# Two units of row lists behind each of three tiles, five listing steps in four expert slots, and two projections moved behind the second sorted tile

## The chip, the core and the metric

The kernel runs on one core of a Trainium2 chip. Its engines are TensorE (PE in the profile; its weight loads are PEld), VectorE (DVE), ScalarE (ACT), GpSimd (POOL) and SyncE (SP). [...] The metric is the device time of one execution in microseconds (us), less is better.

## What is computed

A block with two branches on the same normalised rows, for x of shape (2, 1024, 256):

```
xn = layernorm(x)
out = x + attention(xn) + experts(xn)
```

The attention branch splits every row into 16-channel tokens, projects them to q, k and v, and attends within windows of eight tokens, for half of the channels along one axis and for the other half along the other one, with a small convolution of v added; a projection and a layernorm follow. The expert branch is a mixture of experts:

```
scores = sigmoid(xn @ gate.T);  choose 6 of 16 experts per row (within the best 2 of 4 groups)
for e in experts: out += weight[:, e] * ((silu(xn @ gate_e.T) * (xn @ up_e.T)) @ down_e.T)
out += (silu(xn @ sg.T) * (xn @ su.T)) @ sd.T          # a shared expert for every row
```

An expert has 176 hidden units; there are 2048 rows.

## The kernel before

**Tiles and lists.** The routing is worked out on the chip. The 2048 rows are then sorted so that each of 16 tiles of 128 rows has six experts that most of its rows have chosen. A pair of experts over one tile is a unit of work of the kind "six"; a tile has three such units, and their down projections add up in one PSUM tile. Pairs of row and expert that those six experts do not cover are gathered into 14 lists of 128 rows with one expert each; a pair of lists is a unit of the kind "extra". `units()` (line 1013) lays out the 55 units: the three units of each tile in turn, and behind each of the tiles 7 to 13 one unit of lists.

**The main loop** (from line 1125) runs over `u`, a unit, and `q`, one of its two halves; a half is called an expert slot here, and `i = 2 * u + q` counts them. In slot order the program text issues: a sorted tile that is due (`sorted_tile`, `asked`), a step of the listing, the gathers of the next unit if that is one of lists, then `begun` (up projections of this unit, lines 867 to 870: PE products `pr_u`, Silu on ACT, a multiply on DVE into `hms`), `hidden` of the unit before (L881: three transposes, and an ACT copy), `finished` of the unit two before (down projections, L893 for tiles and L901 for lists, and an ACT copy into `ysum`), then attention steps, and one scatter. A scheduler then reorders instructions on each engine within what their dependences allow, so that the order of an engine is near to that of the text but not the same.

**Lists.** The listing (`lists_begun`) is a generator: three preparing steps, then one step for each of 26 possible lists, then `lists_ended`. A step for list n copies three columns on ACT (`spot`, L967, two buffers), makes two one-hot operands on POOL (L969, L970, in a ring of four), and two steps later a PE product adds it to `rows_of` (L960). One step is taken in every slot from i = 14 on. `lists_ended` writes the row numbers (`lists`, L977 on DVE), which the gathers read. `gathered` (L994) is an indirect DMA that POOL issues, 128 rows into one of the three `xg` buffers; the buffer is free again when the list has been transposed (`turned`, L1001) and its weight column read by the multiply L870. The sorted tiles used the same three buffers before (L827).

**Scatters.** Every finished tile and every finished list is added to the output by an indirect DMA with accumulation (`to_out`, L1008), issued by POOL, 30 in all. Each waits until the one before it has landed, since all write the same output tensor. The attention result is added by eight further DMAs of POOL (L1079).

**Attention steps.** `attention_steps()` yields steps with a cost on DVE and on PE. `walked` takes steps while the DVE count is behind the PE count times a pace. The four parts (two batches, two channel halves) consist each of eight projections (L675 on PE, four copies on ACT L677 to L680), sixteen large DVE operations (L688, L692, L709, L714) and eight transposes (L729); a last stage (L781 to L806) follows. Before the loop, `walked(FIRST_ROWS - LEAD)` takes the first steps of the first part ahead of the second sorted tile; each projection counts 0.3, and so does the gather of rows in front of them. The remaining products of the shared expert (L275, L284, L290) are put behind these by `meanwhile(100)`.

Of the kernel before, what the change touches and what calls it, by code (L numbers as in the profile page):

```python
# [22 lines left out]
P = 128  # L23
# [20 lines left out]
NX = 26  # L44
NL = 14
FIRST = 7
# [5 lines left out]
def csw_block_moe(ctx: ExitStack, tc: tile.TileContext, x, qkv_w, conv_w0, conv_b0, conv_w1, conv_b1,  # L52
# [20 lines left out]
    nc = tc.nc  # L73
# [78 lines left out]
    for c in range(16):  # L152
        n = sum(P // 2 if k % 2 == 0 else P for k in range(c)) + (((16 - c) * P - 1) / 2 if c % 2 == 0 else 0)
# [380 lines left out]
    for c in range(15, -1, -1):  # L534
        n = 16 - c
# [8 lines left out]
        for k in range(1, n):  # L544
            nc.tensor.matmul(down_[:, c + k : c + k + 1], lhsT=beats[:, k, :], rhs=less[:, c % 2 : c % 2 + 1], start=False,
                             stop=(c == 0 and k == 15))
# [25 lines left out]
    for n in range(2):  # L572
        nc.vector.tensor_tensor(ohp[:, 8 * n : 8 * n + 8], row_h.unsqueeze(1).to_broadcast(wide),
                                place[:, 1, 8 * n : 8 * n + 8].unsqueeze(2).to_broadcast(wide), ALU.is_equal)
        for c in range(8 * n, 8 * n + 8):
# [31 lines left out]
    extra = route.tile([NTL, E], F32, name="extra")  # L607
# [6 lines left out]
                     start=True, stop=True)  # L614
# [297 lines left out]
    listed = []  # L912

    def lists_begun():
        flagged = room_[:, 832:960].bitcast(BF16)
        behind = room_[:, 960:1024].bitcast(BF16)
        spot = room_[:, 1024:1280]
        spoti = [t.bitcast(I32) for t in (room_[:, 1280:1536], ysum[:, 7])]
        by_pair = flagged.rearrange("p (e t) -> p e t", t=NTL)
        nc.vector.scalar_tensor_tensor(by_pair, wsrt.rearrange("p t e -> p e t"), 0.0, kept, op0=ALU.is_gt, op1=ALU.mult)  # L920
        nc.vector.tensor_scalar(behind, row_h, part_no, None, op0=ALU.is_gt)
        before = ps_m.tile([P, 2, E * NTL], F32, tag="m", name="before")
        nc.tensor.matmul(before[:, 0], lhsT=behind, rhs=flagged, start=True, stop=True)
        nc.tensor.matmul(before[:, 1], lhsT=ones, rhs=flagged, start=True, stop=True)
        yield
        rows_, some, upto = small.tile([P, E], F32, name="rows_"), small.tile([P, E], I32, name="some"), begin[:, 1]
        nc.vector.tensor_reduce(out=rows_, in_=before[:, 1].rearrange("p (e t) -> p e t", t=NTL), axis=AX.X, op=ALU.add)
        nc.vector.tensor_scalar(some, rows_, P - 1.0, None, op0=ALU.add)
        nc.vector.tensor_scalar(some, some, 7, None, op0=ALU.logical_shift_right)
        nc.vector.tensor_copy(begin[:, 0], some)  # L930
        one_e = one_f.to_broadcast([P, E])
        nc.vector.tensor_tensor_scan(ends, one_e, begin[:, 0], 0.0, op0=ALU.mult, op1=ALU.add)
        nc.vector.tensor_tensor(begin[:, 0], ends, begin[:, 0], ALU.subtract)
        nc.vector.tensor_tensor_scan(upto, one_e, rows_, 0.0, op0=ALU.mult, op1=ALU.add)
        nc.vector.tensor_tensor(upto, upto, rows_, ALU.subtract)
        nc.vector.scalar_tensor_tensor(begin[:, 0], begin[:, 0], float(P), upto, op0=ALU.mult, op1=ALU.subtract)
        nc.vector.tensor_tensor_scan(spot, one_f.to_broadcast([P, E * NTL]), before[:, 1], 0.0, op0=ALU.mult, op1=ALU.add)
        nc.vector.tensor_tensor(spot, spot, before[:, 1], ALU.subtract)
        nc.vector.tensor_tensor(spot, spot, before[:, 0], ALU.add)
        wide = [P, E, NTL]  # L940
        nc.vector.tensor_tensor(spot.rearrange("p (e t) -> p e t", t=NTL), spot.rearrange("p (e t) -> p e t", t=NTL),
                                begin[:, 0].unsqueeze(2).to_broadcast(wide), ALU.add)
        yield
        nc.vector.tensor_copy(spoti[0], spot)
        nc.vector.tensor_scalar(spoti[1], spoti[0], 7, None, op0=ALU.logical_shift_right)
        nc.vector.tensor_scalar(spoti[0], spoti[0], P - 1, None, op0=ALU.bitwise_and)
        nc.gpsimd.memset(at_[:, :, 0:1], 0.0)
        for n in range(2):
            nc.scalar.copy(at_[:, n, 1:], spoti[n])
        nc.vector.tensor_tensor(at_[:, 2, 1:].rearrange("p (e t) -> p e t", t=NTL), by_pair,  # L950
                                of_f.unsqueeze(1).to_broadcast(wide), ALU.mult)
        listed.append(ps_t.tile([P, NX], F32, tag="y1", name="rows_of", padded_shape=[P, TB]))
        yield
        spots = {}
        for n in range(NX + 2):
            if n < NX:
                spots[n] = pair_listed(n)
            if n >= 2:
                spot = spots.pop(n - 2)
                nc.tensor.matmul(listed[0], lhsT=spot[:, 0:P], rhs=spot[:, P:], start=(n == 2), stop=(n == NX + 1))  # L960
            yield
        lists_ended()
        yield

    def pair_listed(n):
        spot = small.tile([P, 3], F32, name="spot", tag="spot")
        nc.scalar.copy(spot, at_[:, :, bass.ds(number(xrow[0:1, 0, n : n + 1], ACT, NTL * E), 1)].rearrange("p a n -> p (a n)"))  # L967
        spots = room_[:, 1024 + 80 * (n % 4) :][:, 0 : (P + NX) // 2].bitcast(F16)
        nc.gpsimd.tensor_scalar(spots[:, 0:P], row_h, spot[:, 0:1], None, op0=ALU.is_equal)  # L969
        nc.gpsimd.tensor_scalar(spots[:, P:], row_h[:, 0:NX], spot[:, 1:2], spot[:, 2:3], op0=ALU.is_equal, op1=ALU.mult)  # L970
        return spots

    def lists_ended():

        none = room_[:, 1500 : 1500 + NX]
        nc.vector.tensor_scalar(none, listed[0], 0.0, ROWS + 1.0, op0=ALU.is_equal, op1=ALU.mult)
        nc.vector.scalar_tensor_tensor(lists[:, 0:NX], listed[0], -1.0, none, op0=ALU.add, op1=ALU.add)  # L977

        over = room_[0:1, 0 : NX * E].rearrange("p (n e) -> p n e", e=E)
        of_list = room_[0:1, 500 : 500 + NX]  # L980
        nc.vector.tensor_tensor(over, ends[0:1].unsqueeze(1).to_broadcast([1, NX, E]),
                                number_f[0:1, 0:NX].unsqueeze(2).to_broadcast([1, NX, E]), ALU.is_le)
        nc.vector.tensor_reduce(out=of_list, in_=over, axis=AX.X, op=ALU.add)
        nc.vector.tensor_scalar(xrow[:, 2, 0:NX], of_list, E - 1.0, None, op0=ALU.min)
        nc.vector.tensor_copy(xrow[:, 1, 0:NX], number_f[0:1, 0:NX])

        some = small.tile([1, 2], F32, name="some_")
        nc.vector.scalar_tensor_tensor(some[:, 0:1], pairs_[0:1], NX + 0.5, pairs_[0:1], op0=ALU.is_gt, op1=ALU.mult)
        nc.vector.tensor_tensor(some[:, 0:1], some[:, 0:1], ends[0:1, E - 1 : E], ALU.max)
        nc.vector.tensor_scalar(left, some[:, 0:1], -float(NL), 0.0, op0=ALU.add, op1=ALU.max)  # L990
# [22 lines left out]
    def units():  # L1013

        six = [[("six", t, k) for k in range(0, TOPK, 2)] for t in range(NTL)]
        for t in range(NTL):
            yield from six[t]
            if FIRST <= t < FIRST + NL // 2:
                yield "extra", 2 * (t - FIRST), 0

    def expert_of(what, q, engine):
        kind, n, k = what
# [61 lines left out]
    of_tile = (0.75, 0.25)  # L1084
    END = 84
    in_walk = [4 * (16 * 2.3 + 3.3 + 2.5 + 1.5 + 1.4) + 0.6 + 8 * 1.4, 4 * 6.2 + 8 * 3.9]
    FIRST_ROWS, LEAD = 2.5, 12
    done = [float(-LEAD), 0.0]
    whole = [in_walk[n] + NTL * TOPK * of_slot["six"][n] + NL * of_slot["extra"][n] + NTL * of_tile[n] for n in range(2)]
    pace = (whole[0] - LEAD - END * of_slot["six"][0] / of_slot["six"][1]) / (whole[1] - END)  # L1090
# [28 lines left out]
    extras_, lists_ = extras_listed(), lists_begun()  # L1119
# [4 lines left out]
    for u in range(len(laid_out) + 2):  # L1124
        for q in range(2):
            i = 2 * u + q

            while tiles_sorted < NTL and 5 * (tiles_sorted - 2) <= 6 * (i - 2):
                sorted_tile(tiles_sorted)
                counted(of_tile)  # L1130
                tiles_sorted += 1
            while len(asked_for) < min(NTL, tiles_sorted + 3):
                asked()
            if i in (2, 4, 8) or i >= 14:
                next(extras_ if i < 14 else lists_, None)
            if u + 1 < len(laid_out) and laid_out[u + 1][0] == "extra":
                n = laid_out[u + 1][1] + q
                ahead[n] = gathered(lists[:, n : n + 1])
            if u < len(laid_out):
                if q == 0:  # L1140
                    fetched(u)
                begun_.setdefault(u, []).append(begun(laid_out[u], q, hms[:, u % 2]))
            if q == 1:
                if 0 <= u - 1 < len(laid_out):
                    hT_[u - 1] = hidden(hms[:, (u - 1) % 2])
                if 0 <= u - 2 < len(laid_out):
                    finished(laid_out[u - 2], hT_.pop(u - 2), wts[:, (u - 2) % 3], begun_.pop(u - 2))
            counted(of_slot[laid_out[min(u, len(laid_out) - 1)][0]])
            walked()
            if done_:  # L1150
                to_out(*done_.pop(0))
            while waiting:
                waiting.pop(0)()
# [73 lines left out]
```

## Time and profile before

| what | us |
|---|---|
| median of three runs (lowest, highest) | 449.53 (446.91, 451.74) |
| the profiled execution: its time | 448.94 |
| the profiled execution: its span | 447.2 |
| PE busy in the span | 393.4 |
| DVE, ACT, POOL busy in the span | 293.0, 215.6, 187.8 |
| scatters L1008: 30, busy on POOL in all | 51.0 |
| gathers L994: 14, busy on POOL in all | 21.2 |

The profile page shows for each engine the busy share in 40 equal slices of the span, then the chain of work that ended last, followed back from the last instruction, then the costliest groups of instructions with what ended the idle time before them. The timeline of an engine lists its instructions in order with the idle time before each and its releaser in square brackets. A table of windows gives the busy time of every engine in a stretch, and the clock that TensorE was granted there, as a share of full speed.

### The profile page before, as it was taken

What the parts mean: (1) busy time and instruction counts of PE and PEld (TensorE: products, weight loads), DVE (VectorE), ACT (ScalarE), POOL (GpSimd) and SP (SyncE); (2) the same over time, 40 slices, a digit from 0 to 9 for tenths busy, and PEclk for the clock granted to TensorE, in tenths of its full rate; (3) what the DMA queues carried; (4) which work ended last, traced back from release to release, by engine and by line L of the source; (5) the groups of instructions that cost most, each with busy time, mean ns of one, the idle gap of its engine ahead of it and who ended that gap; (6) DMA issues with size and microseconds to landing.
All of it is one profiled execution on the core that took longest, in us unless ns stands there. A gap on an engine that the chain in (4) does not pass through costs nothing. (4 is left out here: it accounts for less than half of the span.)

```text
span 447.2 us, 6291 instructions
## 1 busy us (share of the span) xinstructions
PE 393.4 (88%) x1668; PEld 247.4 (55%) x1669; DVE 293.0 (66%) x515; ACT 215.6 (48%) x535; POOL 187.8 (42%) x207
## 2 busy tenths in 40 slices
PE   0999999997887979898898899999899999999970
PEld 0445565655554646665565476566655555666750
DVE  4627958679997948979779599398992333322110
ACT  2955247462472355372462452735335777843220
POOL 7400000220556145886504235324542778791431
PEclk9999999998999999999999699999999999999995
DMA  8999942320423110121012133202331129347222
GB/s 236 314 290 328 272 170 42 48 82 12 86 70 85 22 20 22 33 38 39 22 24 45 52 60 65 44 20 63 85 58 38 22 65 141 74 70 101 44 33 24
DMA packets 40178, 37.56 MB, mean 84 GB/s; under 512 B 5300, under 2 KB 37616, under 8 KB 40112
## 3 DMA queue, kind: packets, MB, share of 16 engines
q0 software_dynamic: 11616, 13.52, 18.4%
q1 hardware_dynamic: 27472, 22.59, 16.6%
q10 hardware_dynamic: 1056, 1.05, 0.7%
q8 instruction: 15, 0.25, 0.2%
q14 instruction: 19, 0.16, 0.1%
HBM read 27.70 MB, written 12.45 MB: 90 GB/s over the span
## 5 line engine op out<-in xcount | busy, mean ns | idle before, releaser
L867 PE MATMUL pr_u<-w1s,xsT 128*128 x384 | 128.3, 468 | 2.7 <-DVE hms L870 2.1
L867 PEld LDWEIGHTS pr_u<-w1s,xsT 128*128 128x128 f32 x384 | 69.9, 190 | 39.3 <-issue 7.1
L1008 POOL DMA_INDIRECT out_dram<-ysum,lists x30 | 51.0, 1701 | 88.5 <-ACT ysum L1047 38.0
L869 ACT ACTIVATE sg<-pr_u 128x176 f32<-128x176 f32 x110 | 34.6, 317 | 83.1 <-PE pr_u L867 73.6
L870 DVE SCALAR_TENSOR_TENSOR hms<-sg,w,pr_u 128x176 f32<-128x176 f32 x96 | 37.4, 392 | 49.1 <-ACT sg L869 46.6
L688 DVE TENSOR_TENSOR pr<-qk 128x2048 f32<-128x2048 f32 x16 | 36.6, 2288 | 15.8 <-ACT qk L677 15.3
L709 DVE TENSOR_TENSOR pv<-s,v 128x2048 f32<-128x2048 f32 x16 | 36.6, 2286 | 4.2 <-ACT s L700 4.2
L692 DVE TENSOR_REDUCE s<-pr 128x256 f32<-128x2048 f32 x16 | 36.5, 2281 | 0.1
L714 DVE TENSOR_REDUCE o<-pv 128x256 f32<-128x2048 f32 x16 | 36.4, 2272 | 0.0
L293 POOL DMA_DIRECT2D out_dram<-ysum x4 | 3.7, 914 | 76.1 <-ACT ysum L291 76.1
L881 PEld LDWEIGHTS ph<-ident,hms 128*128 128x128 f32 x165 | 21.4, 141 | 19.8 <-issue 8.0
L994 POOL DMA_INDIRECT xg<-xw_d,lists x14 | 21.2, 1512 | 26.2 <-DVE hms L870 23.7
L881 PE MATMUL ph<-ident,hms 128*128 128x128 f32 x165 | 29.5, 276 | 2.2 <-DVE hms L870 1.7
L969 POOL TENSOR_SCALAR ysum<-row_h,spot 128x128 f16<-128x128 f16 x26 | 21.3, 825 | 23.4 <-PE rows_of L960 17.0
L827 POOL DMA_INDIRECT xg<-xw_d,lists x16 | 21.6, 1353 | 18.7 <-PE px__1007 L835 6.5
L893 PE MATMUL pr_y<-w2a,hT 128*128 x96 | 28.7, 380 | 0.0
L893 PE MATMUL pr_y<-w2b,hT 112*128 x96 | 28.7, 379 | 0.0
L893 PE MATMUL pr_y<-wts,hT 128*128 128x256 f32 x96 | 28.5, 379 | 0.0
L290 PE MATMUL py<-room 128*128 128x256 f32 x96 | 25.3, 402 | 2.5 <-DVE room L284 2.5
L883 ACT COPY hT<-ph 128x384 f32<-128x384 f32 x55 | 26.3, 479 | 1.9 <-PE ph L881 1.2
L675 PE MATMUL pq<-wq,rows 128*128 128x384 f32 x64 | 24.8, 503 | 2.5 <-ACT oT L731 1.4
L867 PE MATMUL pr_u<-w1s,xd 128*128 x56 | 21.8, 518 | 5.1 <-ACT xd L1003 4.6
(403 smaller groups left out, 703.6 us busy)
## 6 DMA issues: line engine op xcount, KB each, us to landing
w1s<-in_w_dram SPq DMA_DIRECT2D x22, 256.0 KB
wts<-in_w_dram SPq DMA_DIRECT2D x55, 64.0 KB
wts<-in_w_dram SPq DMA_DIRECT2D x55, 48.0 KB
xw_d<-xx SPq DMA_DIRECT2D x4, 544.0 KB
w2a<-in_w_dram SPq DMA_DIRECT2D x4, 512.0 KB
out_dram<-ysum POOLq DMA_DIRECT2D x4, 512.0 KB, 6.8
xr<-xw_d POOLq DMA_DIRECT2D x4, 512.0 KB
out_dram<-att POOLq DMA_DIRECT2D x8, 256.0 KB, 4.1
```

Source lines behind the costliest of these rows:

```text
L290: nc.tensor.matmul(py, lhsT=hms[k, m][:, P * c : P * c + P], rhs=w2h[:, m], start=(m == 0), stop=(m == 2))
L688: nc.vector.tensor_tensor(pr, q_.unsqueeze(3).to_broadcast(full), k_.unsqueeze(2).to_broadcast(full), ALU.mult)
L692: nc.vector.tensor_reduce(out=s[:, n : n + NW], in_=held.pop(n), axis=AX.X, op=ALU.add)
L709: nc.vector.tensor_tensor(pr, s[:, n : n + NW].unsqueeze(3).to_broadcast(full), v[:, br, m : m + NW].unsqueeze(2).to_broadcast(full), ALU. ...
L714: nc.vector.tensor_reduce(out=o[:, n : n + NW], in_=held.pop(n), axis=AX.X, op=ALU.add)
L867: nc.tensor.matmul(pu, lhsT=lhs[:, h, :], rhs=w1s[:, :, h, bass.ds(e * I, I)], start=(h == 0), stop=(h == 1))
L869: nc.scalar.activation(sg, pu[:, 0, :], AF.Silu)
L870: nc.vector.scalar_tensor_tensor(hm[:, 0:I], sg, w, pu[:, 1, :], op0=ALU.mult, op1=ALU.mult)
L881: nc.tensor.transpose(ph[:, s, :], units[:, P * s : P * s + P], ident)
L883: nc.scalar.copy(hT, ph)
L893: nc.tensor.matmul(py, lhsT=l_, rhs=r_, start=start and n == 0, stop=stop and n == 2)
L1008: nc.gpsimd.indirect_dma_start(out=out_rows, out_offset=bass.IndirectOffsetOnAxis(ap=index, axis=0), in_=ys, in_offset=None, bounds_check= ...
```

## The change

There are four edits.

1. `units()` puts one unit of lists behind tile 7 and two behind each of the tiles 8, 9 and 10. The number of units stays 55; the last 15 units are tiles 11 to 15 without lists between them. The two units of lists behind one tile are neighbours.
2. The listing takes a further step in every fourth slot (`i > 16 and i % 4 == 0`), five steps in four slots.
3. The product L960 for a list comes three steps behind its operands instead of two; the ring of four operands stays. With both edits, `lists_ended` is reached in slot 40 instead of 45; the first gathers are still put in slot 46 by the text.
4. `FIRST_ROWS` is 2.0 instead of 2.5: the steps before the loop stop after the gather of rows and six projections instead of eight.

Nothing is computed that was not computed before, and no operation is added or taken away.

```diff
-        for n in range(NX + 2):
+        for n in range(NX + 3):
             if n < NX:
                 spots[n] = pair_listed(n)
-            if n >= 2:
-                spot = spots.pop(n - 2)
-                nc.tensor.matmul(listed[0], lhsT=spot[:, 0:P], rhs=spot[:, P:], start=(n == 2), stop=(n == NX + 1))
+            if n >= 3:
+                spot = spots.pop(n - 3)
+                nc.tensor.matmul(listed[0], lhsT=spot[:, 0:P], rhs=spot[:, P:], start=(n == 3), stop=(n == NX + 2))
             yield
...
+        n = 0
         for t in range(NTL):
             yield from six[t]
-            if FIRST <= t < FIRST + NL // 2:
-                yield "extra", 2 * (t - FIRST), 0
+            for _ in range((t == FIRST) + 2 * (t > FIRST)):
+                if n < NL:
+                    yield "extra", n, 0
+                    n += 2
...
-    FIRST_ROWS, LEAD = 2.5, 12
+    FIRST_ROWS, LEAD = 2.0, 12
...
             if i in (2, 4, 8) or i >= 14:
                 next(extras_ if i < 14 else lists_, None)
+            if i > 16 and i % 4 == 0:
+                next(lists_, None)
```

## The prediction

> **What bounds the kernel now.** I read the 40 slices first, then the end of the chain, then the timelines of PE and POOL where PE stands still, and last the windows around those places. TensorE carries the span: 393.4 of 447.2 us busy, nearly without gaps from slice 1 on.
>
> ```profile
> PE   0999999997887979898898899999899999999970
> PEclk9999999998999999999999699999999999999995
> DMA out_dram<-ysum,lists 3%; POOL out_dram L1008 0%; POOLq L1160 0%; POOLq L1008 0%
> 432.75 0.60 PE L893 MATMUL pr_y<-w2b,hT 112*128 x2
> ```
>
> The chain that ends last is not TensorE's. Its last product ends at 433.35, and 13.85 us follow in which it has no work. POOL fills them:
>
> ```profile
> 397.91 4.79 POOL L1079 DMA_DIRECT2D out_dram<-att  x4
> 408.88 1.66 POOL L1008 DMA_INDIRECT out_dram<-ysum,lists  x1 [6.18 <-ACT sg L869]
> ...
> 435.08 1.54 POOL L1008 DMA_INDIRECT out_dram<-ysum,lists  x1 [1.91 <-DMA out_dram<-ysum,lists]
> 439.61 1.54 POOL L1008 DMA_INDIRECT out_dram<-ysum,lists  x1 [2.99 <-DMA out_dram<-ysum,lists]
> ```
>
> Eight scatters start between 408.88 and 439.61, 4.39 us apart, each waiting for the one before to land. The last sum was ready at about 434.3; its scatter started 5.3 us later, behind a backlog. From there to the end it is 7.59 us.
>
> Inside the span the largest late stop of PE is at the first lists:
>
> ```profile
> 240.64 1.55 POOL L1008 DMA_INDIRECT out_dram<-ysum,lists  x1 [17.68 <-ACT ysum L1047]
> 242.50 2.64 POOL L994 DMA_INDIRECT xg<-xw_d,lists  x1 [0.30 <-issue]
> 247.04 0.69 PE L1001 MATMUL px__2528<-ident,xg 128*128 128x128 f32 x2 [3.09 <-DMA xg<-xw_d,lists]
> 248.37 0.47 PE L1001 MATMUL px__2549<-ident,xg 128*128 128x128 f32 x1 [0.64 <-DMA xg<-xw_d,lists]
> 106.07 1.29 PE L290 MATMUL py<-room 128*128 128x256 f32 x4 [2.52 <-DVE room L284]
> ```
>
> The lists are written at 241.85 (L977), and the first gather stands behind a scatter that waited for its sum. The windows show what comes after such a stop (columns: busy us of PE, PEld, DVE, ACT and POOL, then the granted clock):
>
> ```profile
> 103.50:106.00 2.50, 0.05 (x1) 0.00 (x0) 2.50 (x3) 0.00 (x0) 0.00 (x0) 1.00 0.07 30
> 108.00:110.00 2.00, 2.00 (x5) 1.43 (x5) 1.98 (x3) 0.32 (x1) 0.00 (x0) 0.50 0.00 0
> 249.00:251.00 2.00, 2.00 (x4) 1.25 (x5) 0.43 (x1) 0.00 (x0) 0.00 (x0) 0.50 0.10 24
> ```
>
> **The change part by part**, against the profiled execution (448.94 us, 0.59 under the median). The order of each engine in the changed kernel is known from building it; durations are those of the trace before.
>
> *End.* With no lists behind tiles 11 to 15, only four scatters (tiles 12 to 15) stand behind the last attention DMAs instead of eight. Tiles take PE three units of 4.0 us (405.90 to 409.89), 12 us for each scatter of 4.39, so no backlog is left when PE ends. The last scatter starts 0.9 after PE's last product: 0.9 + 7.6 = 8.5 instead of 13.85, -5.3.
>
> *First lists.* The listing ends five slots sooner, the lists are written about four units before they are needed, and the first three gathers stand behind the scatter of tile 5, not of tile 6. The wait of 3.09 goes. So does what follows it: the first unit of lists took 8.77 us from its first transpose (247.04) to the next unit (255.81), the second 5.77 (268.19 to 273.96). Together -6.1.
>
> *Listing, five steps in four slots.* POOL's two operations take 0.825 + 0.689 = 1.51 on average, five of them and a share of a scatter about 8.8 us, against four slots of 2.2 us (44.2 us for ten units, 171.94 to 216.1). POOL would then have no slack, and ACT, which waits 23.1 us for it at L967 now, waits as often. Against that stand the later product (it waited 1.28 for POOL, once) and two and a half units fewer under listing, whose PE idles 6.3 us between 160.2 and 221. Bounds -3 and +4; I take 0, as this row has both in it.
>
> *Two projections later.* In the new order they stand between the products L290 of the shared expert. The second L688 on DVE needs the last of them: it started at 103.13 and can now start at about 108, some 4.7 us later after taking out the two operations that DVE does meanwhile. DVE has little room here (24.1 of 25 us busy from 100 to 125). Covered by the transposes L729 coming later in PE's order, by one transpose group, one and a half up projections and one unit's down projections, 3.5 us. The stop of 2.52 at L284 stays, shorter or longer by under 1. Bounds -2 and +4; taken +1, the difference. Its DMAs are the same.
>
> *Neighbouring units of lists.* This is the dear part. Four lists follow each other (2 to 5, 6 to 9, 10 to 13), and `xg` has three buffers. The gather of the fourth has to wait until DVE has multiplied the first; behind that gather, on POOL, stand the next scatters and gathers, and on PE everything waits for the fourth list's transposes. PE's order puts these 5.5 us after the first list's products (the rest of that unit, 270.32 to 273.96, then 1.85 for the third list's transposes and products). The gather needs 0.3 of issue, 0.95 to 2.8 on POOL, and 1.95 to land (245.45 + 0.97 to 248.37). If DVE multiplied at once, 0.8 after the products, it would land after 4.0 to 5.9: in time. Two things hold it up:
> - DVE is behind. In its new order three L709, three L714, one L703, L704 and L722 and six multiplies (3 x 2.29 + 3 x 2.28 + 1.21 + 0.94 + 0.69 + 6 x 0.3 = 18.4) stand between the Exp after list 1 and the multiply of list 2, and PE gets from list 1 to list 2 in 16.0 (1.5 + three units of 4.0 to 4.4 + 2.1). Exp ends some 4 us after list 1's products, so DVE is up to 6 late, less what PE itself waits for it. Before list 6 there are eight operations of 2.29, done 4.4 after PE's products.
> - POOL is behind. Before the gather of list 9 come the scatters of tile 8 and lists 2 to 5, before that of list 13 those of lists 6 to 9 and a memset (L757, about 1.3). Scatters with a sum ready stood 4.56 apart among the lists (283.75 after 278.81, for one). From the first of the four sums: 3 x 4.56 + 1.6 + 0.3 = 15.6 to the gather, 18.5 to 20.4 until it has landed; PE is at the fourth transposes after 4.4 + 4.0 + 5.8 + 2.0 - 0.6 = 15.6.
>
> That gives stops of 0 to 6 for list 5 (taken 3.0), 1.9 to 4.8 for list 9 (3.4), and 1.3 to 6 for list 13 (4.1, DVE alone gives 1.3): +10.5.
>
> *The clock after these stops.* In the rows above a stop of 2.5 us was followed by about 3.3 us at half clock (0.73, 0.50 and 0.92 in three windows of 2 us, 1.7 us lost), one of 3.1 by 2.4 us lost (8.77 - 5.77 - 0.64). [...]
>
> Sum: -5.3 - 6.1 + 0 + 1 + 10.5 + 6 = +6.1, so 448.94 + 6.1 = 455.0. What is hidden: the transfers `wts` of SP keep their number and their lead of a unit; the scatters of lists 10 to 13 fall into the attention stage, where POOL has 3.4 us of L801 and L806 in each step of about 6, and three buffers between; if that cover fails, +3.
>
> **The rivals.**
> - *The fourth gathers land in time* (not slower). If DVE reaches the first list's multiply within about 1.5 us of PE's products and the scatters follow each other faster, all three stops and their clock loss go: 448.94 - 5.3 - 6.1 + 1 = 438.5. It decides where the gather can start less than about 2 us after those products. For it: between the lists before, PE never waited for a gather except at the first. Against: there lists came two at a time with two or three units between, and POOL still waited up to 9.2 us for DVE before a gather:
>
> ```profile
> 298.38 2.82 POOL L994 DMA_INDIRECT xg<-xw_d,lists  x1 [9.20 <-DVE hms L870]
> ```
>
> - *Stops without the clock, or one of three missing*: 455.0 - 6 = 449, no change that shows. [...]
> - *Listing at POOL's limit*: ACT stands at L967 ahead of Silu, and PE waits for `hms` in most units under listing; with 4 more there, 459. Against: POOL idled 17 us waiting for PE in the listing before.
> - *The backlog stays*: if the scatters of lists 10 to 13 delay the attention DMAs past 420, the 5.3 are not gained: 460. Against: ten units of tiles follow.
>
> **How the numbers follow.** Stops as summed (or with the listing or backlog cases on top): 0.45, 455.0. Stops in part or without clock loss, near 449: 0.25. No stops, near 438.5, or one small one: 0.30. About 1% of 449.5 (445.0 and 454.0) is what a measurement can tell from no change here, since three runs spread over 4.8 us. Slower by over 1%: 0.45; within: 0.25; faster: 0.30. The range goes from 438, the rival on the other side, to 461, the sum with listing or clock at their upper ends; the likeliest case alone is 450 to 461.
>
> **What would show it.** POOL's last scatter starting about 1 us after PE's last product, and some 8.5 us from there to the end: the end is right. The first L1001 with no wait on its gather: first lists right. Waits of PE at L1001 for `xg` three times, at lists 5, 9 and 13, with POOL's gather before each released by DVE L870 or by a scatter, and clocks near 0.5 behind them: the dear part is right. If these waits are under 1 us, the prediction is wrong and the time is near 439. If PE idles over 8 us under listing, it is wrong about POOL's slack.

## The result and the profile after

The changed kernel takes 464.5 us (median of four runs, 464.11 to 466.25) against 449.49 us (446.91 to 451.74) for the kernel before on the same chip: 1.0374 times as long, 95% interval 1.0339 to 1.0408. The profiled execution took 466.25 us, the longest of the four; its span is 464.4 us, 17.2 more than before, where the medians stand 15.0 apart. 455.0 was predicted, with a range that ended at 461.

The span splits at the last product of PE. Before, it ended at 433.35 and 13.85 us followed; now it ends at 456.52 and 7.9 us follow. So the end of the kernel gained 5.9 us, and everything ahead of it lost 23.2. The timelines of PE and of POOL end with these lines, the last scatter 0.7 us behind the last product, where it stood 6.3 behind it before:

```profile
455.92 0.60 PE L893 MATMUL pr_y<-w2b,hT 112*128 x2
```

```profile
457.20 1.56 POOL L1008 DMA_INDIRECT out_dram<-ysum,lists  x1 [5.37 <-ACTq L1167]
```

PE and its clock in 40 slices, from the page of the changed kernel:

```profile
PE   0999999989787969779899986995974999999993
PEclk9999999999997999998999997997995999999998
```

Each slice is 11.6 us. The clock has a digit of 7 or less in four slices, counted from 1: in slice 13 (7), and in 25 (7), 28 (7) and 31 (5), where PE is low too (6, 5 and 4). PE's timeline has what lies there (in brackets the idle time before the instruction, and what ended it):

```profile
142.22 0.66 PE L835 MATMUL px__1371<-ident,xg 128*128 128x128 f32 x2 [4.37 <-DMA xg<-xw_d,lists]
...
251.97 0.38 PE L1001 MATMUL px__2528<-ident,xg 128*128 128x128 f32 x2
...
283.39 0.66 PE L1001 MATMUL px__2794<-ident,xg 128*128 128x128 f32 x2 [4.27 <-DMA xg<-xw_d,lists]
...
321.64 0.66 PE L1001 MATMUL px__3123<-ident,xg 128*128 128x128 f32 x2 [4.69 <-DMA xg<-xw_d,lists]
...
354.59 0.66 PE L1001 MATMUL px__3378<-ident,xg 128*128 128x128 f32 x2 [7.34 <-DMA xg<-xw_d,lists]
```

The last three are the fourth lists of the three rows of neighbours: `px__2794` is list 5, `px__3123` list 9, `px__3378` list 13, 16.3 us in all. `px__1371` is the gather of a sorted tile, 110 us ahead of the first lists; before, this wait was 1.72. The first lists (`px__2528`) no longer wait.

Each of the four pairs of transposes behind a stop took 0.66 us instead of 0.38: the granted clock has fallen (0.50 from 142.00 to 146.00, behind the first of them). The windows show it for the other three (columns as in the prediction: busy us of PE, PEld, DVE, ACT, POOL, then the granted clock), first inside the stop at list 5, then in the 6 us behind each of the three stops:

```profile
281.39:283.39 2.00, 0.00 (x0) 0.03 (x1) 1.83 (x3) 0.00 (x0) 1.28 (x2) 0.50 0.47 107
...
283.39:289.39 6.00, 6.00 (x19) 4.49 (x20) 0.40 (x1) 1.54 (x4) 1.24 (x2) 0.66 0.14 41
321.64:327.64 6.00, 6.00 (x20) 4.67 (x21) 1.97 (x4) 1.54 (x4) 2.32 (x2) 0.72 0.18 45
354.59:360.59 6.00, 6.00 (x18) 4.50 (x19) 0.40 (x1) 1.54 (x4) 0.00 (x0) 0.62 0.01 3
```

PE is busy all through these 6 us. Clocks of 0.66, 0.72 and 0.62 mean 2.0, 1.7 and 2.3 us lost, 6.0 for the three.

Where the gathers of lists 9 and 13 came from is in POOL's timeline:

```profile
300.65 3.40 POOL L1008 DMA_INDIRECT out_dram<-ysum,lists  x1 [8.98 <-ACT ysum L1057]
306.37 2.68 POOL L1008 DMA_INDIRECT out_dram<-ysum,lists  x1 [2.32 <-DMA out_dram<-ysum,lists]
311.99 2.20 POOL L1008 DMA_INDIRECT out_dram<-ysum,lists  x1 [2.93 <-ACT xd L1003]
316.33 1.56 POOL L1008 DMA_INDIRECT out_dram<-ysum,lists  x1 [2.14 <-DMA out_dram<-ysum,lists]
318.19 1.02 POOL L994 DMA_INDIRECT xg<-xw_d,lists  x1 [0.30 <-DVE s L699]
...
331.34 3.37 POOL L1008 DMA_INDIRECT out_dram<-ysum,lists  x1 [0.30 <-ACT ysum L1057]
337.12 2.51 POOL L1008 DMA_INDIRECT out_dram<-ysum,lists  x1 [2.42 <-ACT sg L869]
342.60 2.62 POOL L1008 DMA_INDIRECT out_dram<-ysum,lists  x1 [2.97 <-ACT xd L1003]
348.08 1.54 POOL L1008 DMA_INDIRECT out_dram<-ysum,lists  x1 [2.85 <-ACT sg L869]
349.06 1.52 POOL L757 MEMSET xe<- 128x1024 f32 x1
350.75 1.07 POOL L994 DMA_INDIRECT xg<-xw_d,lists  x1 [0.17 <-issue]
```

The multiply that frees the buffer of list 9 ended at 315.4 on DVE; its gather started at 318.19, behind four scatters. For list 13 it ended at 344.1, and the gather started at 350.75, behind four scatters and a memset. Six of the eight scatters took 2.2 to 3.4 us; 22 of the kernel's 30 took 1.54 to 1.68. The mean of L1008 over the kernel rose from 1701 to 1937 ns. The next timeline, DVE's in the first of these stretches, shows what ran beside them:

```profile
300.31 2.29 DVE L688 TENSOR_TENSOR pr<-qk 128x2048 f32<-128x2048 f32 x1
302.83 2.28 DVE L692 TENSOR_REDUCE s<-pr 128x256 f32<-128x2048 f32 x1
305.33 2.29 DVE L688 TENSOR_TENSOR pr<-qk 128x2048 f32<-128x2048 f32 x1
```

A scatter that starts while L688 runs ends about 1.4 us after that product: 302.60 and 304.05 for the first, 307.62 and 309.05 for the second. L709 does the same in the other stretch: products from 330.90, 335.91 and 341.52 end at 333.18, 338.20 and 343.81, the scatters at 334.71, 339.63 and 345.22. This became an experiment of its own (the last below).

### The profile page after: what moved, and what is told of

Same layout as the page of the kernel before. It is cut to its first block, busy times and chain, and to the rows that moved or that the text cites. A ratio compares the mean times of both kernels' runs of the same rounds, so it can differ in the third digit from the quotient of the medians.

```text
span 464.4 us, 6299 instructions
## 1 busy us (share of the span) xinstructions
PE 399.0 (86%) x1668; PEld 251.6 (54%) x1669; DVE 293.1 (63%) x515; ACT 216.3 (47%) x535; POOL 191.0 (41%) x207
## 3 DMA queue, kind: packets, MB, share of 16 engines
q0 software_dynamic: 11616, 13.52, 17.5%
## 4 chain that ended last, share of the span: by engine, by line
PE 34%; DVE 20%; DMA 18%; issue 11%; POOL 11%; ACT 4%; POOLq 0%; DVEq 0%; SPq 0%; ACTq 0%
DMA out_dram<-ysum,lists 7%; PE pr_u L867 7%; DVE o L714 5%; DVE pv L709 5%; PE py L290 4%; PE pg L275 4%; PE pr_y L893 4%; PE pu L275 3%; DMA xr<-xw_d 3%; DMA xg<-xw_d,lists 3%; DVE hms L870 3%; POOL att L806 3%; PE pq L675 2%; PE pp L781 2%; POOL ysum L970 2%
## 5 line engine op out<-in xcount | busy, mean ns | idle before, releaser
L867 PE MATMUL pr_u<-w1s,xsT 128*128 x384 | 130.4, 473 | 4.5 <-DVE hms L870 3.9
L1008 POOL DMA_INDIRECT out_dram<-ysum,lists x30 | 58.1, 1937 | 113.1 <-ACT ysum L1050 55.2
L867 PEld LDWEIGHTS pr_u<-w1s,xsT 128*128 128x128 f32 x384 | 71.1, 193 | 41.7 <-issue 8.9
L870 DVE SCALAR_TENSOR_TENSOR hms<-sg,w,pr_u 128x176 f32<-128x176 f32 x96 | 37.2, 394 | 65.9 <-ACT sg L869 65.8
L688 DVE TENSOR_TENSOR pr<-qk 128x2048 f32<-128x2048 f32 x16 | 36.6, 2290 | 15.5 <-ACT qk L677 15.1
L709 DVE TENSOR_TENSOR pv<-s,v 128x2048 f32<-128x2048 f32 x16 | 36.6, 2286 | 4.8 <-ACT s L700 4.8
L969 POOL TENSOR_SCALAR ysum<-row_h,spot 128x128 f16<-128x128 f16 x26 | 27.4, 1076 | 24.7 <-ACT spot L967 11.7
L881 PE MATMUL ph<-ident,hms 128*128 128x128 f32 x165 | 32.3, 288 | 5.5 <-DVE hms L870 4.9
L881 PEld LDWEIGHTS ph<-ident,hms 128*128 128x128 f32 x165 | 22.5, 148 | 23.4 <-DVE hms L870 8.5
L893 PE MATMUL pr_y<-w2a,hT 128*128 x96 | 30.6, 402 | 0.0
L827 POOL DMA_INDIRECT xg<-xw_d,lists x16 | 21.2, 1325 | 22.3 <-DVE hms L870 8.1
L893 PE MATMUL pr_y<-wts,hT 128*128 128x256 f32 x96 | 29.6, 391 | 0.0
L290 PE MATMUL py<-room 128*128 128x256 f32 x96 | 24.1, 388 | 2.2 <-DVE room L284 2.2
L994 POOL DMA_INDIRECT xg<-xw_d,lists x14 | 18.7, 1336 | 16.9 <-DVE hms L870 13.5
```

The costliest lines, as they stand in the source:

```text
L290: nc.tensor.matmul(py, lhsT=hms[k, m][:, P * c : P * c + P], rhs=w2h[:, m], start=(m == 0), stop=(m == 2))
L688: nc.vector.tensor_tensor(pr, q_.unsqueeze(3).to_broadcast(full), k_.unsqueeze(2).to_broadcast(full), ALU.mult)
L709: nc.vector.tensor_tensor(pr, s[:, n : n + NW].unsqueeze(3).to_broadcast(full), v[:, br, m : m + NW].unsqueeze(2).to_broadcast(full), ALU. ...
L867: nc.tensor.matmul(pu, lhsT=lhs[:, h, :], rhs=w1s[:, :, h, bass.ds(e * I, I)], start=(h == 0), stop=(h == 1))
L870: nc.vector.scalar_tensor_tensor(hm[:, 0:I], sg, w, pu[:, 1, :], op0=ALU.mult, op1=ALU.mult)
L881: nc.tensor.transpose(ph[:, s, :], units[:, P * s : P * s + P], ident)
```

## The experiments

The kernel before had a median of 449.89 us when the first four of these kernels were measured, and of 448.94 with the next four. Ratios are to it, with 95% intervals.

**Each part alone.** The three parts of the change were put into the kernel before one at a time. First the order of units:

```diff
+        n = 0
...
-            if FIRST <= t < FIRST + NL // 2:
-                yield "extra", 2 * (t - FIRST), 0
+            for _ in range((t == FIRST) + 2 * (t > FIRST)):
+                if n < NL:
+                    yield "extra", n, 0
+                    n += 2
```

> The kernel before with the new order of units alone; listing and projections as before. Theory A (four neighbouring lists on three xg buffers): three waits of PE for a gather at lists 5, 9 and 13 of 3 to 8 us each and some 2 us of slow clock behind each, 20 us or more in all; the end gains about 6; the wait at the first lists stays at about 3. Time 458 to 465 us. Theory B (the faster listing makes most of the loss, the stops come from its shifting of POOL): this kernel stays near 449, and its stops are under 2 us each.

Measured: 466.51 us, ratio 1.0355 (1.0316 to 1.0395). PE's waits (us in total, times, longest):

```profile
PE px__3378 L1001 <- DMA xg<-xw_d,lists: 7.7, 1, 7.7
PE px__3123 L1001 <- DMA xg<-xw_d,lists: 4.7, 1, 4.7
PE px__2794 L1001 <- DMA xg<-xw_d,lists: 4.3, 1, 4.3
PE px__2528 L1001 <- DMA xg<-xw_d,lists: 3.1, 1, 3.1
```

This is 1.5 us above what theory A gave. The three stops come with the order alone, at the same lists and of nearly the same size, and the wait of 3.1 at the first lists stays. The order of units by itself costs 16.6 us, its shorter end included.

Then the listing:

```diff
-        for n in range(NX + 2):
+        for n in range(NX + 3):
...
+            if i > 16 and i % 4 == 0:
+                next(lists_, None)
```

> The kernel before with five listing steps in four slots and the product three steps behind; units and projections as before. Theory A: the wait at the first lists (about 6 us with its slow clock) goes, and the stretch under listing costs 3 to 7 us more than its work, as in the changed kernel; the eight scatters at the end stay. Time 446 to 451. Theory B (the listing is the large loss): 455 or more.

Measured: 444.6 us, ratio 0.9902 (0.987 to 0.9935), 5.3 us faster, and below the range of theory A. The first lists start without a wait:

```profile
244.27 0.38 PE L1001 MATMUL px__2528<-ident,xg 128*128 128x128 f32 x2
```

The listing did not slow anything that shows: the first transposes L729 of the first part stand at 159.44 (160.23 before).

Then the two projections:

```diff
-    FIRST_ROWS, LEAD = 2.5, 12
+    FIRST_ROWS, LEAD = 2.0, 12
```

> The kernel before with FIRST_ROWS at 2.0 alone. Theory A: the second L688 starts near 108 instead of 103, and PE's first group of transposes L729 comes about 5 us later with 3.5 us more work done before it: 450 to 452. Theory C (the early lag of DVE is carried through and is a large part of the loss): 454 or more.

Measured: 454.99 us, ratio 1.014 (1.0075 to 1.0206), 5.1 us slower; theory C. DVE's timeline of this run at the first part of attention:

```profile
108.25 2.29 DVE L688 TENSOR_TENSOR pr<-qk 128x2048 f32<-128x2048 f32 x1 [5.31 <-ACT qk L677]
```

DVE stands idle for 5.31 us, waiting for the copies of the two projections that were moved. It gets back only part of this: its second L688 starts 5.1 us later than before (103.13), and an L709 at 136.52 is still 3.0 later (133.49). The windows of 10 us of this run (third number: DVE):

```profile
100.00:110.00 10.00, 8.14 (x33) 5.95 (x32) 4.69 (x4) 3.63 (x13) 1.76 (x2) 1.00 0.14 22
110.00:120.00 10.00, 8.64 (x37) 5.43 (x36) 10.00 (x9) 3.62 (x11) 4.08 (x3) 1.00 0.41 88
...
130.00:140.00 10.00, 7.14 (x33) 4.65 (x33) 10.00 (x20) 4.41 (x9) 6.24 (x4) 0.99 0.31 64
```

Before, DVE was busy 9.84 us of the first of these windows, and 9.4 to 9.9 in the next three. It is DVE that has no room here, and PE that has (7 to 9 of 10 us busy). PE even gains at first: its stop at L284 is shorter (1.86 us instead of 2.52), no half clock follows it (1.00 in the first window, 0.85 before), and the up projections that stood between 112 and 139 before now start 1.2 to 4.6 us earlier. It pays later, where it needs what DVE releases:

```profile
136.59 3.09 POOL L827 DMA_INDIRECT xg<-xw_d,lists  x1 [0.30 <-DVE hms L870]
141.69 0.66 PE L835 MATMUL px__1371<-ident,xg 128*128 128x128 f32 x2 [4.45 <-DMA xg<-xw_d,lists]
225.81 1.09 PE L729 MATMUL po<-ident,xo 128*128 128x128 f32 x8 [1.57 <-DVE xo L722]
```

DVE's multiply L870, now late, frees a buffer; the gather L827 behind it lasts 3.09 us beside a product L709 (136.52 to 138.79), and PE stops for it at `px__1371`, 4.45 us instead of 1.72, with a clock of 0.5 in the 4 us behind it. The first half of these:

```profile
141.69:143.69 2.00, 2.00 (x6) 1.39 (x7) 0.95 (x3) 0.50 (x2) 0.83 (x2) 0.50 0.49 130
```

That this gather meets the product right at its start is bad luck, worth 2.1 of the 3.09 us by the 0.95 to 1.0 that the gathers of 138.86 to 141.43 took in the kernel before. There PE falls from 2.6 us ahead to 1 to 2 behind. From the second part's transposes on, which wait for DVE's `xo`, it is 4.8 behind, and from the second pair of lists to its last product 6.1. The changed kernel has the same stop at 142.22.

The three parts alone add up to 16.6 - 5.3 + 5.1 = 16.4 us. The whole change cost 15.0.

**A fourth buffer.** If the stops are a matter of three buffers for four neighbouring lists, a fourth one takes them away. Room for it came from a small constant, which now shares a buffer of another tile:

```diff
-        xg = work.tile([P, ROW], F32, tag="xg", name="xg", bufs=3)
+        xg = work.tile([P, ROW], F32, tag="xg", name="xg", bufs=4)
```

> The changed kernel with four xg buffers instead of three (a row of ones moves to another pool to make room). Theory A: POOL issues the fourth gather ahead of the scatters, the three waits of PE (16.3 us in the changed kernel) and the slow clock behind them (about 6) go, and the end stays as in the changed kernel: 441 to 446. Theory D (the gathers are late because POOL and its queue are full of scatters, buffers or not): the waits stay over 2 us each and the time is over 455.

Measured, the changed kernel with four buffers: 447.72 us, ratio 0.9917 (0.9869 to 0.9965), 16.8 us less than the changed kernel and 1.7 above the forecast of 441 to 446. Its ten runs lie apart, three at 442.3 to 443.1 us, one at 446.0 (the profiled one) and six at 447.6 to 449.0; why is open. (The ratio is one of means, so it is lower than that of the medians.) No wait at L1001 for a gather is left. The gather of list 5 no longer needs the buffer of list 2; it was issued at 257.66, behind that of list 4. In its old place POOL's timeline has the gathers of lists 6 to 9 (the two in the middle are left out below), so that list 9 too is asked for before the scatters, 35 us earlier than in the changed kernel:

```profile
276.19 3.12 POOL L994 DMA_INDIRECT xg<-xw_d,lists  x1 [1.34 <-DVE hms L870]
...
283.09 0.95 POOL L994 DMA_INDIRECT xg<-xw_d,lists  x1 [0.30 <-issue]
284.34 1.62 POOL L1008 DMA_INDIRECT out_dram<-ysum,lists  x1 [0.30 <-issue]
```

The fourth buffer serves the sorted tiles too, and the stop at `px__1371` is gone as well in this run. Yet its first transposes L729 come at 163.09, so the lag of the projections is not that one stop: DVE still waits 4.1 us for the copies of the moved projections.

**Without the projections' move.** The same with `FIRST_ROWS` back at 2.5:

> The changed kernel with a fourth xg buffer and FIRST_ROWS back at 2.5 (listing and units of lists stay). Theory A (the projections' lag of 5.1 us is a cost of its own, independent of the stops): 447.7 - 5.1 = 442.6, between 440 and 445; no stop above 1 us at the lists; the second L688 of the first part starts near 103, not 108. Theory B (with the stops gone the lag falls into slack that the fourth buffer leaves): 446 to 449. Theory C (the shorter end is worth its full 5.3 us once the stops are gone): 444.6 (listing alone) - 5.3 = 439.3.

Measured: 440.33 us (439.23 to 442.9), ratio 0.9818 (0.977 to 0.9867). This is the fastest kernel of the study, 1.8% faster than the one before. The lag is a cost of its own (theory A, though the time is nearer to the 439.3 of theory C than to 442.6): the first L729 stands at 157.23, 5.9 earlier than with the projections moved, PE's last product 5.9 earlier, and the span is 6.0 shorter. Without the stop PE pays in steps: with the projections moved its up projections are 1.2 us later at 143, 5.0 at 174 and 6.4 at 215. (The medians, 7.4 apart, hold the spread of the run before.)

**What the order of units is worth without its stops.** The listing edits and four buffers, with the lists one unit behind each tile as before:

> The kernel before with the listing edits and a fourth xg buffer; one unit of lists behind each tile, as before. Theory A (a fourth buffer only cures what the neighbouring units broke; the order of before has no stop at a list): the same as the listing alone, 443 to 446. Theory B (a fourth buffer gains by itself, and the gain of the four-buffer run was not the cure of the stops): 438 to 441. Set against e5 it tells what the earlier lists are worth without their stops: 2 us or less by theory A of e5, 5 by theory C.

Measured: 443.52 us (441.79 to 444.33), ratio 0.9881 (0.9847 to 0.9915). Against the listing alone (444.6) the fourth buffer does nothing that can be told from nothing. Against the run before this one: its tail behind PE's last product is 13.3 us, that of the run with neighbouring units 8.0, and its PE ends at 426.7 instead of 430.1. So the new order gains 5.3 at the end, as forecast, and gives 3.4 back on the way, even without stops: 1.9 us are left by these two profiles, 3.2 by the medians, between the two theories. PE's waits name 2.2 of these: `pr_u` waits for the ACT copy of the transposed list (`xd`, L1003) 13 times with 7.3 us in all, instead of 10 times with 5.1. It may be that two units of lists side by side leave less other work to put between a transpose and its product; no run tested this.

**Earlier lists, not neighbouring ones.** One unit behind each of the tiles 6 to 12, three buffers, listing edits:

```diff
-FIRST = 7
+FIRST = 6
```

> The kernel before with the listing edits and FIRST = 6: one unit of lists behind each of the tiles 6 to 12, three buffers. Single units, so by theory A (stops come only from neighbouring units) no stop at lists 5, 9 and 13; the first gathers are put in slot 40, in which the listing ends, so the first lists wait 2 to 6 us; nine units stand behind the last lists instead of six, which takes 2 to 4 us off the end: 442 to 447 in sum. Theory B (the stops come from the lists being early, while attention still loads DVE): stops of 3 us or more at several lists, 452 or more.

Measured: 446.54 us (444.12 to 451.08), ratio 0.997 (0.9939 to 1.0002). No list waits for its gather, not even the first, where 2 to 6 us were expected; the stops belong to neighbouring units and not to lists being early. But the end was misjudged: 12.3 us behind PE's last product (13.9 in the run with the listing alone), though nine units of tiles follow the last lists. POOL's timeline:

```profile
401.93 4.74 POOL L1079 DMA_DIRECT2D out_dram<-att  x4
413.00 1.65 POOL L1008 DMA_INDIRECT out_dram<-ysum,lists  x1 [6.33 <-ACT sg L869]
...
434.72 1.54 POOL L1008 DMA_INDIRECT out_dram<-ysum,lists  x1 [2.95 <-DMA out_dram<-ysum,lists]
```

The attention DMAs come 4 us later than in the kernel before (397.91), and the six scatters behind them still follow each other at the pace of their landing, 4.3 us on average, until the end. Here the fewer scatters at the end gained 1.6 us, with the queue still full; in the changed kernel, where it had run empty, 7.9 us follow PE's last product.

**POOL's queue or the buffer.** The changed kernel, three buffers, without the lists' scatters, so that the lists' rows are missing from its output:

```diff
-                done_.append((ys, lists[:, n + q : n + q + 1]))
```

> The changed kernel, three buffers, without the 14 scatters of the lists (their rows are not added to the output); the 16 scatters of tiles stay. Tells POOL's queue from the buffer. Theory A (list 5 waits for its buffer, which L870 on DVE frees; lists 9 and 13 stand behind scatters in POOL's queue, by 2.8 and 6.6 us after their buffer is free): the stop at list 5 stays at 3.5 to 4.5, that at list 9 falls to 1 to 3, that at list 13 to 0 to 2, sum 5 to 9 instead of 16.3. Theory B (the buffer alone): three stops of 4 or more. Theory C (POOL's queue alone): all three below 1. Time by A about 448 to 455, the end without the last scatter included.

Measured: 458.52 us (454.91 to 458.85), and in PE's waits:

```profile
PE px__2788 L1001 <- DMA xg<-xw_d,lists: 4.2, 1, 4.2
...
PE px__3105 L1001 <- DMA xg<-xw_d,lists: 2.0, 1, 2.0
...
PE px__3348 L1001 <- DMA xg<-xw_d,lists: 1.6, 1, 1.6
```

Theory A in all three numbers. Of 16.3 us, 8.5 came from scatters standing ahead of the gathers in POOL's queue; 7.8 are the buffer, freed by DVE, and the gather itself, which at list 5 again took 3.11 us (at list 13 a memset of 0.95 us still stands between the free buffer and the gather). The time is 3.5 us above the forecast of 448 to 455. PE ends 10.05 us earlier (446.47), but the tail is 10.4 instead of 7.9: from the issue of the last scatter to the end of the span it is 9.7 instead of 7.2. Why is open.

**A scatter beside a product on DVE.** Five stages of six scatters, without the block around them (shortened; the stage of sums begins with one product, which the sums read):

```
def stage(dve):
    nc.vector.tensor_copy(ys, src)      # waits for the last scatter of the stage before
    for n in range(6):
        scatter()                       # accumulates ys into 128 rows of the output
    large_operations(dve)               # twelve on DVE, of 128x2048 elements, or none
for dve in ("none", "both", "sums", "products", "none"):
    stage(dve)
```

> Not the block: five stages of six accumulating scatters of 128 rows into the output, each waiting for the one before it, while DVE does nothing (stage 1), alternates products like L688 and sums like L692 (2), makes sums alone (3), products alone (4), and nothing again (5). Theory A (an issue on POOL that meets a product of two SBUF operands on DVE cannot finish until some 1.4 us after the product's end; a sum does not hold it): 1.5 to 1.7 us for each scatter in stages 1, 3 and 5, a mean of 2.2 to 3.4 in stage 2, and in stage 4 more than in stage 2, 3 to 6. Theory B (any large DVE operation lengthens it): stages 2, 3 and 4 alike. Theory C (it is no matter of DVE, but of the other transfers and POOL work in the kernel): 1.5 to 1.7 in all five. The spacing follows: 4.4 to 4.7 where nothing holds the issue, 5.2 or more in stage 2 by theory A.

Measured, by stage: 1.54 to 1.67 us for each scatter with DVE idle; in the second stage a mean of 2.16, just under the 2.2 to 3.4 that theory A gave (the scatters stand 4.81 apart there, not 5.2 or more); in the stage of sums 1.54, all six; with products alone 1.54 to 1.95, a mean of 1.77. POOL's timeline has these among the scatters of the second stage, and the first one of the third:

```profile
34.71 3.63 POOL L103 DMA_INDIRECT out_dram<-ys,at  x1 [2.94 <-DVE qk L108]
40.79 1.54 POOL L103 DMA_INDIRECT out_dram<-ys,at  x1 [2.45 <-DMA out_dram<-ys,at]
44.77 2.36 POOL L103 DMA_INDIRECT out_dram<-ys,at  x1 [2.44 <-DMA out_dram<-ys,at]
...
63.38 1.54 POOL L103 DMA_INDIRECT out_dram<-ys,at  x1 [3.07 <-DVE qk L108]
```

DVE's timeline at the same times (the row of the sums holds two, their time added up):

```profile
34.63 2.29 DVE L96 TENSOR_TENSOR pr<-qk 128x2048 f32<-128x2048 f32 x1
39.04 4.47 DVE L100 TENSOR_REDUCE s<-pr 128x256 f32<-128x2048 f32 x2
43.43 2.28 DVE L96 TENSOR_TENSOR pr<-qk 128x2048 f32<-128x2048 f32 x1
63.37 2.34 DVE L96 TENSOR_TENSOR pr<-qk 128x2048 f32<-128x2048 f32 x1
```

The product of 34.63 ends at 36.92, the scatter that met it at 38.34; that of 43.43 ends at 45.71, its scatter at 47.13. The scatter at 40.79 lies beside a sum and takes 1.54. So the product holds the issue and the sum does not (theory A against B and C). Theory A's figure for the fourth stage, 3 to 6 us, was wrong: the hold ends with the product that the scatter met, although the next product follows at once. The scatter at 109.83 there ends at 111.78, 1.42 after its product (108.08 to 110.36). So the price was what was left of that one product, 2.1 us at most here (3.63 less 1.54).

One thing limits this. The scatter at 63.38 started 0.01 us after its product and took 1.54, and so did the first one of the fourth stage: they were not held. (At this distance both happen: the gather at 137.11 in the changed kernel, as close behind an L709, took 3.16.) Further into a product the hold was regular. In all eleven traces together, 66 scatters and 64 gathers of POOL started more than 0.03 us into one of DVE's products L688, L699, L709 and L722 (L96 here) and more than 0.02 before its end. Every gather ended 0.82 to 0.92 us after the product, and every scatter 1.41 to 1.53 after it, save four that met an L722 next and ended 1.42 to 1.49 after that. None of the 75 scatters that started beside a sum or a maximum took more than 1.65 us.

So the hold is measured; what makes it is not shown. A product differs from a sum here by its larger output too (128x2048 against 128x256).

## Why the prediction was wrong in size

The direction was right, and so were the places: the prediction named the stops at lists 5, 9 and 13, what releases their gathers, and half clocks behind them. By its own steps:

- *End*, -5.3: measured -5.9 (13.85 to 7.9), and -5.3 between the two runs with four buffers. Right.
- *First lists*, -6.1, and *Listing*, 0: together -5.3 in the run with the listing alone, and its stop is gone. Right in sum; no run parts the two.
- *Two projections later*, +1: measured +5.1 alone, and 5.9 to 6.0 between the two profiles with four buffers. **This step failed.** It let 3.5 us of PE work cover a delay of 4.7 us on DVE. The row that it quoted, DVE busy 24.1 of 25 us from 100 to 125, said already that the delay was on the engine without room. PE did get ahead at first, by 2.6 us and more, but DVE stayed 3 to 5 us late, and PE lost it all where it next needed DVE: a late buffer, a gather held by a product, a stop of 4.45 us with half clock behind it, then the transposes of the second part. A hole of 5.3 us in DVE came out as 5.1 us of time, and without that stop, with four buffers, as no less. The upper bound of that step, +4, was too low as well.
- *Neighbouring units*, +10.5 as 3.0, 3.4 and 4.1: measured 16.3 as 4.3, 4.7 and 7.3. **The mechanism was right and this term was too small by 5.8.** The scatters were taken 4.56 us apart; ahead of list 13 they stood 5.58 apart (348.08 - 331.34 over three), which makes 3.1 of the 3.8 us by which the gather came later than summed (19.4 instead of 15.6 after the first scatter); the memset, which the sum of 15.6 leaves out, makes most of the rest. For list 9 it was 17.5 us from the first scatter to the gather against 15.6. At list 5 the gather took 3.12 on POOL, above the bound of 2.8, and landed 2.5 after it. In all of these POOL met products of DVE, which held its issues: the three long scatters ahead of list 13 took 3.9 us more than three of 1.54. The trace of before had this. The pair that the prediction names for its 4.56 (278.81 and 283.75) stands 4.94 apart, and a pair beside products in that trace 5.19:

```profile
304.64 2.16 POOL L1008 DMA_INDIRECT out_dram<-ysum,lists  x1 [2.17 <-ACT ysum L1047]
309.83 2.31 POOL L1008 DMA_INDIRECT out_dram<-ysum,lists  x1 [3.02 <-DMA out_dram<-ysum,lists]
```

  Three of 5.19 and the 1.9 of that sum are 17.5, what list 9 measured. By the printed sum the lower end for list 9 is also 2.9 (18.5 - 15.6), not 1.9.
- *The clock after these stops*, +6: measured 6.0. The 6 was an estimate, 2.0 for each of three stops, between the 1.7 and 2.4 us that the trace of before shows behind its stops of 2.5 and 3.1; it held. The three stops were all longer than those, 4.3 to 7.3 us. What shorter ones bring is in the other traces. In those of the ten kernels, later than 90 us, all 14 stops of PE of 3.09 us or more have a spell at half clock of 6.8 or 10.2 us that starts in them or within 1.5 us behind; of 14 stops of 2.17 to 2.65 us, 9 have one of 3.4 us; of 23 stops of 1.5 to 2.0 us, 3 have, the shortest of 1.58 us at list 13 without the lists' scatters:

```profile
345.23:347.23 2.00, 2.00 (x8) 1.82 (x9) 0.00 (x0) 0.85 (x2) 0.00 (x0) 0.50 0.00 0
```

  So a half clock came behind 9 of the 14 stops of about 2.5 us, and not behind the other 5.
- Not in the sum: the neighbouring units' waits for the ACT copies, part of the 3.4 us that the runs with four buffers show. In the changed kernel itself they are 4.8 us, against 4.6 before, and explain none of its loss.

With measured terms the sum is -5.9 - 5.3 + 5.1 + 16.3 + 6.0 = +16.2, against 17.2 us between the two spans. The two terms that were too small, by 4.1 and 5.8, are 9.9 of the 11.1 us by which this differs from the +6.1 forecast. Of the rivals, *the fourth gathers land in time* is what the fourth buffer brings about: that run has no stop, and its time lies 9 us above the 438.5 given for this rival, mostly because that figure held the same +1 for the projections and nothing for the copies.

## What to carry to other kernels

Before work is moved, ask which engine has no room in that stretch: here a delay on that engine was paid in full, and what another engine did meanwhile was no cover. Where units that borrow buffers are put side by side, count the buffers against the length of the run, and what the queue issues between the free buffer and the next request; here one more buffer turned 3.7% slower into 0.8% faster, and with the projections left alone into 1.8% faster. Take the durations of POOL's DMA issues from a stretch with the same work on DVE: here a scatter took 1.54 to 1.65 us beside sums and up to 3.63 beside products.

## What was not expected of the hardware

- An indirect DMA issue of POOL took 0.94 to 1.04 us (gather, beside a sum in the traces of before and after) or 1.54 to 1.67 us (scatter, with DVE idle or summing in the run without the block). When it started more than 0.03 us into one of the products L688, L699, L709, L722 or L96 on DVE, a gather ended 0.82 to 0.92 us and a scatter 1.41 to 1.53 us after that product, the four scatters aside that met an L722 next: up to 3.4 us in the changed kernel and 3.63 in the run without the block.
- Accumulating scatters that follow each other into one tensor stood 4.0 to 4.5 us apart with DVE idle in the run without the block, 4.4 on average at the end of the kernel before, and 4.3 to 6.3 in the changed kernel beside attention from 262.58 to 348.08, the longest from 267.21 to 273.48.
- In the traces of the ten kernels, later than 90 us: of 37 stops of PE of 1.5 to 2.65 us, 12 came with a spell of 3.4 us at half clock; all 14 of 3.09 us or more came with one of 6.8 or 10.2 us.
